# Query columns from a side-by-side head layout by SyncE, and an output projection in four quarters

## The chip, the cores and the metric

The kernel runs on one core of one Trainium2 chip. The metric is the time of one execution on the device in microseconds (us); shorter is better. A core has five instruction streams: TensorE (PE) multiplies matrices, VectorE (DVE) and ScalarE (ACT) do elementwise work, GpSimd (POOL) does small elementwise work and gathers, and SyncE (SP) only issues memory transfers (DMAs). Each stream runs in its own order; semaphores hold an instruction until what it needs is there. ACT and POOL can issue DMAs too, and an instruction that waits holds everything behind it on its engine.

## The reference

There are 64 sequences of 32 tokens with 512 features. Two residual layers are computed, all in float32:

```
W = weights[condition]                                  # 16 matrices of 32 x 32, one per sequence
x = x + einsum('bct,bcd->bdt', x, W)
q = rope(rmsnorm(x Wq^T)), k = rope(rmsnorm(x Wk^T)), v = x Wv^T      # 32 query heads, 8 key heads of 128
k_all = [k_cache[block_table] (512 keys), k],  v_all likewise         # 16 pages of 32 keys
scores = q k_all^T / sqrt(128); cached keys beyond the sequence's length are masked
x = x + (softmax(scores) v_all) Wo^T
```

## The kernel before, in words

Four sequences make a tile of 128 token rows, so there are 16 tiles. The 8 key heads are split in two halves of 4, and the kernel goes through all tiles for the first half and then for the second: 32 **steps**, numbered 0 to 31. A step has 4 **batches** (its sequences), a batch 4 **slots** (its key heads), so a step has slots 0 to 15. The second half adds to what the first half left in memory (`acc_d`).

A slot of attention is: `scores` (L806, 8 matmul records, an exponential on ACT into `pr`), and `values` of the slot before (L865, 8 matmul records into `po`). A slot with nothing else is called bare here. Slots 0, 1 and 3 of a step also do the 32 new keys (`new_scores` into `psn`, `new_values` into `pnv`).

Cached keys come as 16 pages a batch, one DMA of 64 KB each, issued by SP (`load_k`, L308) into one of two buffers `k_t`. DVE copies one head's keys at a time into `kh` (`head_keys`, L794), three slots ahead of its use. A buffer is free for the next batch but one when its fourth head is copied, which is the copy made in the batch's first slot. Cached values are gathered by POOL into `raw` and masked by ACT into `v` (L362).

Beside the attention of a step, the queries, keys and values of later tiles are made. From step 4 on, two tiles form a pair (`Pair`, L602), and the projections of both are computed together in block products (`products`, L661, seven products in place of eight, in the manner of Strassen and Winograd). There are three sets: set 0 (query heads 0 and 1) and set 1 (2 and 3) are made in the even step two steps ahead of the pair, set 2 (keys and values) in the odd step after. Each set has four parts, `p1_p6`, `p5_p2`, `p7` and `p4_p3`, and a list of four slots says where each stands (`where`, L1221). A set needs three sums of weights, `t2`, `t3` and `t4`, of 512 KB. They are made once in each half and then loaded by SP from `sums_d` for each pair (`load_sums`, L655), two buffers in turn (tile `t_x` in the profile). Each product's result goes through `norm_rope` (L466: squares on ACT, a reduction on DVE, a power on POOL, five more operations on DVE) and through a transposition on DVE in blocks (`turn_rows`, L513), and POOL writes it to memory (`heads_d`).

From there the rows come back as columns (`spread`, L524): one step ahead, 4 DMAs of 240 KB bring the first three batches' columns into `q_cols` and 4 DMAs of 80 KB the last batch's into `q_last` (two buffers). The `q_cols` DMAs are issued by ACT, the `q_last` DMAs by SP (`spread_of`, L1144). `q_cols` has one buffer, whose last reader is slot 11.

After a batch, DVE turns its output (`turn`, L899) into `ot`, and one step later the output projection multiplies `ot` with `Wo` in 16 matrix products (`out_proj`, L742), 8 in slot 8 and 8 in slot 9; DVE adds the result to the residual tile `res`, and SP stores it at slot 11 (`store`, L761).

The order of PE and of SP is the order of the program text, which the loop over steps and slots (L1283) and the table `plan` make; on DVE, ACT and POOL a scheduler of the framework places the instructions. In a slot the program has: the scores, the planned pieces, the output projection, the fetch of values, the values, and the key copies. A batch's key pages are issued at the start of the batch two ahead of it; those of the batch that starts in slot 12 are issued half there and half at slot 13. All DMAs of SP and ACT take eight semaphores in turn, in program order, and each DMA waits for the one eight before it.

## Time and profile before

| what | value |
|---|---|
| median of 3 runs | 2630.88 us (2629.29 to 2639.11) |
| the profiled execution's own time | 2618.95 us |
| its span, from the first to the last instruction | 2617.2 us |
| mean granted TensorE clock | 0.915 of full speed |
| DMA | 478.66 MB, mean 183 GB/s |
| key pages | 2048 DMAs of 64 KB by SP |
| weight sums loaded | 108 DMAs of 512 KB by SP |
| head rows written | 150 DMAs of 256 KB by POOL, 2.8 us to landing |
| columns loaded | 120 DMAs of 240 KB by ACT, 120 of 80 KB by SP |

How to read it. A line of the engine summary gives the busy time, its share of the span and the number of instructions; PEld is PE's weight load, which overlaps PE. A line of waits reads "engine line <- what it waited for: us in total, times, longest". SPq and ACTq are the parts of these engines that issue DMAs, which do not count as busy. A line of a timeline gives start and duration in us, engine, line of the kernel, operation, what it writes and reads (buffer numbers left out), the shape, how many instructions are merged, and in brackets how long the engine was idle before and what ended that. Where such a line names a DMA or an engine, it is the last of several semaphores that were waited for. A line of queues gives packets, MB and the time the packets took as a share of the 16 DMA engines' span; q1 belongs to SP, q10 to ACT, q0 to POOL. The profile is of one execution.

### The profile page before, as it was taken

What the parts mean: (1) busy time and instruction counts of PE and PEld (TensorE: products, weight loads), DVE (VectorE), ACT (ScalarE), POOL (GpSimd) and SP (SyncE); (2) the same over time, 40 slices, a digit from 0 to 9 for tenths busy, and PEclk for the clock granted to TensorE, in tenths of its full rate; (3) what the DMA queues carried; (4) which work ended last, traced back from release to release, by engine and by line L of the source; (5) the groups of instructions that cost most, each with busy time, mean ns of one, the idle gap of its engine ahead of it and who ended that gap; (6) DMA issues with size and microseconds to landing.
All of it is one profiled execution on the core that took longest, in us unless ns stands there. A gap on an engine that the chain in (4) does not pass through costs nothing.

```text
span 2617.2 us, 42090 instructions
## 1 busy us (share of the span) xinstructions
PE 2205.8 (84%) x12804; PEld 1546.5 (59%) x12804; DVE 1365.4 (52%) x3142; ACT 863.2 (33%) x1591; POOL 903.4 (35%) x1089
## 2 busy tenths in 40 slices
PE   8999888797887978878888797887978879788788
PEld 5765565565655656655565565665656656555566
DVE  4657756455464553745646355373453734537423
ACT  3442433233432333223333233332333323332242
POOL 3533434234342342423334233232332423324221
PEclk9999899898998988999889898898988989889989
DMA  7765665665656656676766865655656566565563
GB/s 223 216 180 171 194 201 171 176 199 176 195 165 179 197 170 193 203 223 177 217 180 187 217 184 170 184 163 173 193 167 190 163 175 191 166 183 162 165 182 95
DMA packets 485755, 478.66 MB, mean 183 GB/s; under 512 B 57072, under 2 KB 400496, under 8 KB 485520
## 3 DMA queue, kind: packets, MB, share of 16 engines
q1 hardware_dynamic: 368016, 262.22, 35.2%
q0 software_dynamic: 55088, 180.01, 21.9%
q10 hardware_dynamic: 62416, 33.64, 5.3%
q8 instruction: 105, 1.72, 0.3%
q14 instruction: 130, 1.06, 0.1%
HBM read 406.45 MB, written 69.21 MB: 182 GB/s over the span
## 4 chain that ended last, share of the span: by engine, by line
PE 55%; DMA 19%; SPq 10%; issue 5%; DVE 4%; ACT 2%; POOL 2%; ACTq 0%; POOLq 0%; DVEq 0%
PE pout_x L749 14%; PE ps_x L810 11%; PE po_x L871 11%; SPq L322 10%; PE pb_x L671 8%; DMA k_t_x<-in_kt_dram 6%; DMA t_x<-sums_d 6%; PE pc_x L671 5%; DMA q_cols_x<-heads_d 4%; PE pa_x L671 4%; PE pp_q_x L461 1%; DVE kh_x L803 1%; ACT sq_q_x L471 1%; PE psn_x L831 1%; DMA raw_x<-in_vc_dram,v_row 1%
## 5 line engine op out<-in xcount | busy, mean ns | idle before, releaser
L349 POOL DMA_INDIRECT raw_x<-in_vc_dram,v_row x512 | 540.9, 1057 | 937.9 <-ACT v_x L362 865.4
L871 PE MATMUL po_x<-v_x,pr_x 128*128 128x129 f32 x4088 | 584.4, 287 | 214.4 <-ACT pr_x L821 113.9
L871 PEld LDWEIGHTS po_x<-v_x,pr_x 128*128 128x128 f32 x4088 | 542.7, 200 | 351.1 <-issue 121.2
L821 ACT ACTIVATE pr_x<-ps_x 128x512 f32<-128x512 f32 x511 | 306.3, 599 | 1036.6 <-PE ps_x L810 1025.1
L749 PE MATMUL pout_x<-wo_x,ot_x 128*128 128x512 f32 x1024 | 450.1, 592 | 0.0
L810 PE MATMUL ps_x<-q_cols_x,kh_x 128*128 128x128 f32 x3064 | 420.5, 282 | 10.0 <-DMA q_cols_x<-heads_d 9.1
L362 ACT ACTIVATE v_x<-raw_x,valid 128x512 f32<-128x512 f32 x512 | 367.2, 721 | 144.6 <-DMA k_t_x<-in_kt_dram 51.8
L810 PEld LDWEIGHTS ps_x<-q_cols_x,kh_x 128*128 128x128 f32 x3064 | 387.7, 198 | 14.3 <-issue 13.5
L671 PE MATMUL pb_x<-t_x,x_x 128*128 128x512 f32 x432 | 245.2, 697 | 145.2 <-DMA t_x<-sums_d 145.1
L803 DVE COPY kh_x<-k_t_x 128x512 f32<-128x512 f32 x506 | 212.5, 421 | 256.3 <-PE ps_x L810 244.8
L749 PEld LDWEIGHTS pout_x<-wo_x,ot_x 128*128 128x128 f32 x1024 | 191.9, 190 | 228.2 <-issue 227.9
L671 PEld LDWEIGHTS pb_x<-t_x,x_x 128*128 128x128 f32 x432 | 87.3, 223 | 236.7 <-issue 226.0
L687 DVE TENSOR_TENSOR u_x<-pb_x,z_x 128x512 f32<-128x512 f32 x84 | 58.0, 691 | 291.1 <-PE pb_x L671 280.7
L478 POOL TENSOR_TENSOR rs_q_x<-ms_q_x,minus_half 128x4 f32<-128x4 f32 x128 | 143.2, 1119 | 154.6 <-DVE ms_q_x L476 153.3
L889 DVE TENSOR_TENSOR nv_x<-po_x,nv_x 128x258 f32<-128x258 f32 x256 | 107.0, 418 | 152.8 <-PE po_x L871 145.3
L475 DVE TENSOR_REDUCE ms_q_x<-sq_q_x 128x4 f32<-128x512 f32 x128 | 87.2, 681 | 157.8 <-ACT sq_q_x L471 157.5
L522 POOL DMA_DIRECT2D heads_d<-rows_x x150 | 91.0, 607 | 188.7 <-DVE rows_x L517 86.2
L810 PE MATMUL ps_x<-q_last_x,kh_x 128*128 128x128 f32 x1024 | 148.0, 292 | 0.0
L810 PEld LDWEIGHTS ps_x<-q_last_x,kh_x 128*128 128x128 f32 x1024 | 137.5, 209 | 0.0
L365 POOL COPY v_x<-valid 128x16 f32<-128x16 f32 x128 | 32.1, 251 | 265.2 <-PE po_x L871 265.0
L892 DVE TENSOR_TENSOR o_x<-nv_x,rden 128x256 f32<-128x256 f32 x256 | 107.5, 420 | 5.9
L671 PE MATMUL pc_x<-wq_x,x_x 128*128 128x512 f32 x224 | 105.9, 595 | 0.0
(180 smaller groups left out, 2126.5 us busy)
## 6 DMA issues: line engine op xcount, KB each, us to landing
k_t_x<-in_kt_dram SPq DMA_DIRECT2D x2048, 64.0 KB
t_x<-sums_d SPq DMA_DIRECT2D x108, 512.0 KB
heads_d<-rows_x POOLq DMA_DIRECT2D x150, 256.0 KB, 2.8
q_cols_x<-heads_d ACTq DMA_DIRECT2D x120, 240.0 KB
q_last_x<-heads_d SPq DMA_DIRECT2D x120, 80.0 KB
sums_d<-t SPq DMA_DIRECT2D x18, 512.0 KB
raw_x<-in_vc_dram,v_row POOLq DMA_INDIRECT x512, 4.0
wo_x<-in_wo_dram SPq DMA_DIRECT2D x32, 256.0 KB
```

The costliest lines, as they stand in the source:

```text
L322: ins = nc.sync.dma_start(k_raw[:, j, :, :].rearrange("p g r -> p (g r)"), kt[hh, bass.ds(page[j], 1)].rearrange("o d e -> (o d) e"),)
L349: nc.gpsimd.indirect_dma_start(out=raw.rearrange("p g d -> p (g d)"), out_offset=None, in_=vc, in_offset=bass.IndirectOffsetOnAxis(ap=v_ro ...
L362: nc.scalar.activation(v_bufs[b % 2][:, c, :, 0:D], raw, AF.Copy, scale=ok)
L478: nc.gpsimd.tensor_tensor(rs, ms, minus_half, ALU.pow)
L671: nc.tensor.matmul(bank, pair.x[:, i, c, :], w[:, c * 512 : (c + 1) * 512], start=start and c == 0, stop=c == 1, skip_group_check=not start,)
L749: nc.tensor.matmul(st.po, st.ot[:, i, :], wt["o", st.hh, i // 4][:, i % 4, :], start=(i == 0), stop=(i == QH - 1),)
L803: last["dve"] = nc.vector.tensor_copy(k, ba.k_raw[:, :, g, :]).ins
L810: nc.tensor.matmul(ps[:, c, :], ba.k[g][:, c * P : (c + 1) * P], queries(ba, g), start=True, stop=True,)
L821: last["act"] = nc.scalar.activation(pr, ps, AF.Exp, scale=SCALE).ins
L871: nc.tensor.matmul(ba.po[:, g % 2, :], ba.pr[g][:, c, :], ba.v_t[:, c, g, :], start=(c == 0), stop=(c == VC - 1),)
L889: nc.vector.tensor_tensor(t, ba.po, t, ALU.add)
L892: nc.vector.tensor_tensor(ba.o[:, both, :], t[:, :, 0:D], rd.unsqueeze(2).to_broadcast([P, 2, D]), ALU.mult,)
```

## The change

The memory layout of a step's heads changes from rows that hold four 128-element blocks of one head each to `[4, 128, 5, 128]`: for each of the four blocks, and for each of its 128 (batch, element) rows, the five heads (four query heads and the key head) stand side by side. POOL's write of one head becomes 128 x 4 pieces of 512 bytes in place of 128 rows of 2048. A column load becomes pieces of 5 x 512 = 2560 bytes in place of 512, and all of them are issued by SP: the `q_cols` loads move from ACT to SP.

The columns of a pair's first tile are now loaded in slot 14 (`q_cols`) and 15 (`q_last`) in place of 13 and 14, those of the second tile in slots 13 and 10 in place of 12 and 10. The sets move to slots 4, 6, 8, 9 (set 0), 11 to 14 (set 1) and 4, 6, 8, 11 (set 2), and loads of weight sums, of the pair's inputs and of weights move with them. From step 4 on the output projection goes in quarters into slots 5, 7, 8 and 10. The turning of the first two batches moves from slot 9 to 10, that of the third stays in slot 13, and the store moves from 11 to 13.

```diff
--- before.py
+++ after.py
@@ -198,7 +197,7 @@
         for hh in range(NHH)
     ]
     heads_d = [
-        dram.tile([HEAD_ROWS, 4 * P], F32, tag=f"heads_d{n}", name=f"heads_d{n}")
+        dram.tile([4, P, GH + 1, P], F32, tag=f"heads_d{n}", name=f"heads_d{n}")
         for n in range(NHH * NT)
     ]
 
@@ -378,8 +377,8 @@
             tag = "acc"
             if st.n in (2, 3, 5) and not exact:
                 tag = "sums"
-            elif st.n > 7 and not exact:
-                tag = ("u3", "u2")[st.n % 2]
+            elif st.n > 6 and st.n % 2 and not exact:
+                tag = "u3"
             st.acc = work.tile(
                 [P, HID], F32, tag=tag, name=f"acc_{st.name}", bufs=1 if tag[0] == "u" else 2
             )
@@ -518,21 +517,16 @@
                 part.rearrange("p k (h s) -> p h k s", h=4),
                 rd.rearrange("p h (k d) -> p h k d", k=4),
             )
-            rows = heads_d[st.n][i * S : i * S + (GH + 1) * P : GH + 1, :]
-            nc.gpsimd.dma_start(rows, part.rearrange("p k c -> p (k c)"))
-
-        def spread(st, b0, b1, eng):
-
-
-            whole_rows = heads_d[st.n]
+            nc.gpsimd.dma_start(heads_d[st.n][:, :, i, :].rearrange("k p c -> p k c"), part)
+
+        def spread(st, b0, b1):
+
+
+            src = heads_d[st.n].rearrange("k (b d) i c -> k d b (i c)", b=BT)
+            to = q_last[st.n % 2].unsqueeze(1) if b0 == BT - 1 else q_cols
+            to = to.rearrange("p b i c -> p b (i c)")
             for k in range(4):
-                src = bass.AP(
-                    tensor=whole_rows.tensor,
-                    offset=whole_rows.offset + b0 * (GH + 1) * S * 4 * P + k * P,
-                    ap=[[(GH + 1) * 4 * P, S], [S * 4 * P, (b1 - b0) * (GH + 1)], [1, P]],
-                )
-                to = q_last[st.n % 2] if b0 == BT - 1 else q_cols.rearrange("p b i c -> p (b i) c")
-                eng.dma_start(to[k * S : (k + 1) * S], src)
+                nc.sync.dma_start(to[k * S : (k + 1) * S], src[k][:, b0:b1, :])
 
         def by_tensor(st):
             return st.n < 2 or exact
@@ -693,7 +687,7 @@
             t = {}
 
             def p1_p6():
-                t[2], t[3] = made[pair.hh, k] if first else (pair.t[k, 0], pair.t[k, 1])
+                t[2] = made[pair.hh, k][0] if first else pair.t[k, 0]
                 b11, t["b21"], t[1], t["b22"] = halves(pair.hh, k)
                 t["a"], t["b"] = bank("pa"), bank("pb")
                 product(t["a"], A11, b11, True)
@@ -712,7 +706,7 @@
                 done(s0, e0, t["a"])
 
             def p7():
-                product(t["b"], S3, t[3])
+                product(t["b"], S3, made[pair.hh, k][1] if first else pair.t[k, 1])
                 t["u3"] = temp("u3")
                 add(t["u3"], t["b"], t["z"])
                 if e1[0] == "v":
@@ -1142,12 +1136,8 @@
                 at(n, slot, work_of)
 
         def spread_of(st, cols, last_cols):
-            def by_scalar():
-                with tc.issue_after(last["act"]):
-                    spread(st, 0, BT - 1, nc.scalar)
-
-            at(st.n - 1, cols, by_scalar)
-            at(st.n - 1, last_cols, lambda: spread(st, BT - 1, BT, nc.sync))
+            at(st.n - 1, cols, lambda: spread(st, 0, BT - 1))
+            at(st.n - 1, last_cols, lambda: spread(st, BT - 1, BT))
 
         def angles_of(m, n, slot):
             def angles():
@@ -1202,7 +1192,7 @@
             elif not pair.hh:
                 at(n - 1, 12, lambda pair=pair: pair_x(pair))
                 input_of(s0, n - 1, (n - 1, 9), (n - 1, 6), 12, 13)
-                input_of(s1, n - 1, (n - 1, 10 if n > 4 else 12), (n - 1, 7), 14, 15)
+                input_of(s1, n - 1, (n - 1, 11 if n > 4 else 12), (n - 1, 7), 14, 15)
                 at(n, 1, lambda pair=pair: sums_x(pair))
                 angles_of(s0.n // 2, n - 1, 9)
                 tables_of(pair, "q", n, 1)
@@ -1210,40 +1200,41 @@
             else:
                 at(
                     n - 1,
-                    10 if n < NT else 10,
+                    12,
                     lambda pair=pair: pair_x(pair),
                     lambda pair=pair: load_x(pair),
                 )
-                at(n - 1, 13, lambda pair=pair: sums_x(pair))
+                at(n, 1, lambda pair=pair: sums_x(pair))
                 tables_of(pair, "q", n - 1, 11)
                 tables_of(pair, "k", n + 1, 2)
             if early:
                 where = [(0, 2, (10, 11, 12, 14)), (1, 3, (4, 5, 6, 8)), (2, 3, (9, 10, 11, 12))]
             else:
                 where = [
-                    (0, n, (4, 5, 6, 8)),
-                    (1, n, (10, 11, 12, 14)),
-                    (2, n + 1, (4, 5, 6, 8)),
+                    (0, n, (4, 6, 8, 9)),
+                    (1, n, (11, 12, 13, 14)),
+                    (2, n + 1, (4, 6, 8, 11)),
                 ]
             for k, m, slots in where:
                 fresh = early or half_first
                 set_of(pair, k, m, slots, fresh)
                 if fresh:
-                    at(m, slots[0] - 2, lambda pair=pair, k=k: sums_w(pair.hh, k))
+                    before = 1 if k == 1 and not early else 2
+                    at(m, slots[0] - before, lambda pair=pair, k=k: sums_w(pair.hh, k))
                 else:
                     at(m, slots[0] - 2, lambda pair=pair, k=k: load_sums(pair, k, 0))
-                    at(m, slots[0] - 1, lambda pair=pair, k=k: load_sums(pair, k, 1))
-                    at(m, slots[1], lambda pair=pair, k=k: load_sums(pair, k, 2))
-            spread_of(s0, 13, 14)
-            spread_of(s1, 12, 10)
+                    at(m, slots[0] - (k != 1), lambda pair=pair, k=k: load_sums(pair, k, 1))
+                    at(m, slots[0] + 1, lambda pair=pair, k=k: load_sums(pair, k, 2))
+            spread_of(s0, 14, 15)
+            spread_of(s1, 13, 10)
         for i in range(2):
             for g in range(2):
-                at(NT - 4, 9 + 2 * g + i, lambda i=i, g=g: load_parts([("q", g)], 1, i))
+                at(NT - 4, 10 + 2 * g + i, lambda i=i, g=g: load_parts([("q", g)], 1, i))
         for j in range(4):
             g, i = 2 + j // 2, j % 2
             at(NT - 4 + (j > 0), 15 if j == 0 else j - 1, lambda g=g, i=i: load_parts([("q", g)], 1, i))
             kind = "kv"[j // 2]
-            at(NT - 3, 9 + j, lambda kind=kind, i=i: load_parts([(kind, 0)], 1, i))
+            at(NT - 3, 12 + j, lambda kind=kind, i=i: load_parts([(kind, 0)], 1, i))
 
         def count(hh):
 
@@ -1272,6 +1263,7 @@
         load_cond_weights(2)
         for part in (3, 4, 5):
             load_parts(outputs, 0, part)
+        out_parts = [{8: (0, 1), 9: (2, 3)}, {5: (0,), 7: (1,), 8: (2,), 10: (3,)}]
         second_outputs = {
             (0, 10): (0,),
             (1, 2): (1,),
@@ -1305,15 +1297,15 @@
                     kept.clear()
                     if slot == 3 and st.n > 2:
                         reload(steps[st.n - 1])
-                    if slot in (8, 9) and st.n:
-                        out_proj(steps[st.n - 1], slice((slot - 8) * QH // 2, (slot - 7) * QH // 2))
-                    if slot == 9:
+                    for part in out_parts[st.n > 3].get(slot, ()) if st.n else ():
+                        out_proj(steps[st.n - 1], slice(part * GH, (part + 1) * GH))
+                    if slot == 10:
                         if st.n:
                             new_ot(st)
                         for ba in turned:
                             turn(ba)
                         turned = []
-                    if slot == 11 and st.n:
+                    if slot == 13 and st.n:
                         store(steps[st.n - 1])
                     if slot == 13:
                         for load in after.pages_left if after else ():
@@ -1332,7 +1324,7 @@
                     if slot >= GH and valued is not None:
                         values(*valued)
                     valued = this, g
-                    if g == 1 and bt != 1:
+                    if g == 1 and bt in (0, BT - 1):
                         for ba in turned:
                             turn(ba)
                         turned = []
```

More of the change, by code (lines that the diff above doesn't have):

```diff
@@ L54 @@
 WARM = 10
-HEAD_ROWS = (GH + 1) * (P + S)
 TRIG = 2
```

## The prediction

> **What bounds the kernel now.** I read the page's busy times first, then the waits of PE and of SP, then the timelines of one pair of steps (20 and 21) engine by engine.
>
> ```profile
> PE 2205.8 (84%) x12804; PEld 1546.5 (59%) x12804; DVE 1365.4 (52%) x3142; ACT 863.2 (33%) x1591; POOL 903.4 (35%) x1089
> ...
> PE pb_x L671 <- DMA t_x<-sums_d: 145.1, 26, 11.3
> PE po_x L871 <- ACT pr_x L821: 113.9, 16, 11.3
> PE po_x L871 <- ACT v_x L362: 100.4, 15, 8.4
> ...
> SPq L322 <- DVE kh_x L803: 647.9, 84, 18.0
> ```
>
> PE is the bound, and its 411 us of idle time are nearly all in these three waits: 214.3 us on ACT (31 waits, 7 us each) and 145.1 us on weight sums. What ACT does meanwhile stands in its timeline; the first two lines are the end of odd step 19, the others even step 20:
>
> ```profile
> 1657.71 10.01 ACTq L535 DMA_DIRECT2D q_cols_x<-heads_d  x4
> 1667.77 0.72 ACT L362 ACTIVATE v_x<-raw_x,valid 128x512 f32<-128x512 f32 x1 [9.56 <-DMA k_t_x<-in_kt_dram]
> ...
> 1734.80 10.71 ACTq L535 DMA_DIRECT2D q_cols_x<-heads_d  x4
> 1745.61 0.63 ACT L471 ACTIVATE sq_q_x<-u_x 128x512 f32<-128x512 f32 x1 [10.24 <-DMA k_t_x<-in_kt_dram]
> ```
>
> Four column loads hold ACT for 10 us, though each issue takes 310 ns (median over the line's 120). The rest is waiting for the landing of key pages: ACT's loads stand in one order with SP's pages and cannot pass them. PE in the same two places, then at the next weight sum:
>
> ```profile
> 1669.03 2.09 PE L871 MATMUL po_x<-v_x,pr_x 128*128 128x129 f32 x8 [7.94 <-ACT pr_x L821]
> 1672.33 2.05 PE L810 MATMUL ps_x<-q_cols_x,kh_x 128*128 128x128 f32 x8 [1.22 <-DMA q_cols_x<-heads_d]
> ...
> 1746.91 0.80 PE L871 MATMUL po_x<-v_x,pr_x 128*128 128x129 f32 x2 [8.05 <-ACT v_x L362]
> ...
> 1778.62 3.75 PE L671 MATMUL pb_x<-t_x,x_x 128*128 128x512 f32 x4 [9.61 <-DMA t_x<-sums_d]
> ```
>
> So a pair has three stalls: B, at the end of the odd step (7.94 + 1.22); A, in slot 13 of the even step (8.05); C, in slot 4 of the next odd step (9.61). After each, the matmuls run at half speed for a while (x8 in 2.09 instead of 1.05). The pair repeats every 164 us. What C hangs on is in DVE's and SP's timelines:
>
> ```profile
> 1746.28 0.69 DVE L475 TENSOR_REDUCE ms_q_x<-sq_q_x 128x4 f32<-128x512 f32 x1 [4.94 <-ACT sq_q_x L471]
> ...
> 1761.92 0.40 DVE L803 COPY kh_x<-k_t_x 128x512 f32<-128x512 f32 x1
> ...
> 1770.61 0.91 SPq L456 DMA_DIRECT2D rot_k_x<-rot_dk  x2
> 1771.62 0.84 SPq L658 DMA_DIRECT2D t_x<-sums_d  x2
> ```
>
> DVE is behind with four rope chains; the key copy that frees the page buffer comes only at 1762.3. SP then issues 16 pages (8.3 us), two rope tables and the weight sum, which PE gets 7.0 us after its issue.
>
> **Part 1, stall A: column loads of odd steps, from ACT to SP.** I measure from the slot in which the second block set begins (scores at 1723.02, slot 10) to the end of C (1778.62): 55.6 us. In the new kernel this set begins in slot 11. Its PE work up to the next step is five slots, 5.2 + 5.2 + 3.5 + 5.2 + 1.8 = 20.9 us (bare slot 1.8, a pair of products 1.7, in the same timeline). But PE doesn't end the stretch. The built program's order for DVE has the same rope chains in front of the key copy that frees the buffer. In the old trace DVE runs from 1733.56 (first reduction of the set's ropes, 10.5 after the set's start) to 1762.32: 28.8 us, of which 4.94 waiting for ACT and 0.94 + 0.60 for POOL, so 22.3 of work. In the new order one key copy (0.4) now comes before this stretch and one addition and reciprocal (0.5) behind it: 21.4. With the two POOL waits kept the copy ends at 10.5 + 21.4 + 1.5 = 33.4 us, and C ends 16.3 us later (1762.32 to 1778.62), at 49.7. Since one bare slot now lies before the set, the gain is 55.6 - 49.7 - 1.8 = 4.1 us, not the 8 of the stall with its slow matmuls: PE is there at 20.9 + 13.2 (slots 0 to 4) = 34.1 and loses 15 us, some 3 at late key copies, which is new, and 12 in C. Bounds: if DVE catches up, PE alone sets the end, a gain of 19.7; if POOL's or ACT's answers cost DVE another 5 us, a loss of 1. I take 4.1, because the copy order is known and the ropes are the same. The new wait that the squeezed slots 11 to 14 could make, on the third weight sum behind 8 pages (4.2 us), is at most 2 us and lies before the same copy. Even steps 4 to 28 are 13; step 14 is followed by no load of sums and keeps all (its slots 13 and 14 last 7.5 and 7.6 us, against 3.5 and 5.2: 6.4). So 12 x 4.1 + 6.4 = 56.
>
> Step 30 has no products; its 8.4 us stall becomes a wait for columns behind 8 pages: 1.5 + 4.2 + 1.7 + 4.9 landing = 12.3 against 7.2 of PE work. Gain 11 - 5 = 6. Steps 2 and 3 stall 5.8 and 2.2 on ACT; I take half, 4.
>
> **Part 2, stall B: column loads of even steps.** Here SP issues them behind 16 pages. Before, from the scores of slot 12 (1654.67) to the first scores of step 20 (1672.33): 17.7 us for 7.2 us of PE work. After: key copy 1.5, 16 pages 8.4 to 10.0 (8.23 to 10.01 in the rows), output store 0.4, in the second half the two inputs of the next pair (now in slot 12) 0.9, four column loads at SP's median 0.43 = 1.7, landing 4.9 (1667.41 to 1672.33): 16.5 to 19.4. That is the old 17.7. ACT is free, but PE's next scores need these very columns. In the second half 0.75 MB more (inputs and store) lie before them, 3.7 us at the 202 GB/s of that stretch if nothing else gives; the larger pieces give about 1 back. I take +1 us for 7 odd ends and -1 us for 6: 1 us lost. Ends: -2 to +4 us for each of 15.
>
> ```profile
> 1655.00:1672.00 17.00, 8.17 (x63) 7.68 (x61) 4.19 (x11) 4.95 (x9) 4.89 (x6) 0.78 0.84 202
> ```
>
> (Stretch, its length, busy time of PE, weight loads, DVE, ACT, POOL, granted clock, DMA share, GB/s.)
>
> **Part 3, the pieces.**
>
> ```profile
> q1 hardware_dynamic: 368016, 262.22, 35.2%
> q0 software_dynamic: 55088, 180.01, 21.9%
> q10 hardware_dynamic: 62416, 33.64, 5.3%
> ```
>
> The ACT queue with its 512-byte pieces moves 33.64 MB in 5.3% of 2617, 242 GB/s; POOL's queue, with 2 KB rows, 314. The columns (39 MB) go from the first rate to the second or better, 162 to 125 us of all engines; the head writes, now 512 pieces of 512 bytes instead of 128 of 2 KB, go the other way by the same 37. Sum 0. POOL's issue of 512 pieces is shown by wk_x at 788 ns against 607: 150 x 0.18 = 27 us on an engine busy 35%. What hides it is POOL's idling; without that, a rope's power on POOL comes 0.2 us later, inside the 1.5 us above.
>
> SP gets 120 issues, 51 us, and waits 648 us for key copies, which hides them, except at B, where they are counted. The other moves (the later input by a slot, weight loads at the half change by one to three, weight sums by a slot, x4 issues each or fewer) stay in stretches where SP waits for key copies: 0, and without that cover 0.4 us for each issue, some 2 us a pair. The stores at slot 13 wait for nothing: the projection ends in slot 10. Turning two batches in slot 10 instead of 9 fits, since the projection first reads them in the next step.
>
> **Part 4, the projection in quarters.** 32 matmuls of 0.43 us either way, 13.7 us a step: 0 in PE time. It fills bare slots, so the key pages keep pace there; the old trace shows no PE wait for keys to win back. The price is that the first set's four ropes now end on the second set's heels; I counted about 4 us of DVE slack before the second set, so 0. Were it gone, each 1 us costs 12.
>
> **A rule against the change.** ACT's row is 10.01 us for four issues of 0.31. The Trainium skill, DMA: Bandwidth & Descriptors, section "Issuing engines are not separate DMA queues", says that queues of several engines share the same 16 DMA engines and that issuing from another one saves only sequencer time. By it the move would save ACT 1.24 us a step, none of it on PE's path, and the sum would be 0; by the row it also takes 9 us of waiting off ACT. For B I side with the rule's result, for A with the row.
>
> **Sum.** 56 + 6 + 4 - 1 = 65 us. The profiled execution took 2618.95 (span 2617.2), so 2554; the median of the three runs is 2630.88, 12 above it, so 2566.
>
> **Rivals.**
> - *DVE catches up* (0.17): without ACT's hold the ropes start early enough and C shrinks too; 3 to 6 us more in each of 13 pairs is 2566 - 39 to 78 = 2488 to 2527. Against it: 21 us of rope work in 20.9 us of slots.
> - *The change only moves the wait* (0.08): DVE's lag takes 5 us in each even step; 2618 to 2644.
> - *SP as the new neck, slower* (0.13): the columns wait in one in-order queue behind 16 pages, inputs and a store. From 5.2 us for each of 15 odd ends it is slower (65 gained and 13 of uncertainty); at 8 us it gives 2566 + 120 = 2686. For it: the DMA share is 0.84 there already. Against: SP has finished its pages at 1666.2, and ACT's last load went out at 1667.4, so the time is the same.
>
> **Numbers.** My forecast has 0.62, with a range of its own of 2527 to 2617. Faster by over 0.5%, which is about what a measurement tells from no change: 0.62 + 0.17 = 0.79; same 0.08; slower 0.13. The range 2505 to 2625 leaves out the slower case and the lower part of the first rival.
>
> **What will show it.** PE's waits on ACT pr_x and v_x fall from 214 us to under 60, and no ACT row is ended by a key page. PE's wait on t_x stays at 120 to 200, and on q_cols_x it rises from 9 to about 130, at the first scores of even steps. DVE's busy time stays near 1365. I am wrong if the odd ends grow beyond 21 us, if the key copies stop PE by more than 4 us in a pair beside C, or if C falls below 6.

## The result, and the profile after

The changed kernel takes 2622.23 us (median of 17 runs, 2612.49 to 2634.74); the kernel before, run beside it, 2628.55 us (17 runs, 2618.94 to 2639.11). The ratio is 0.9976 with a 95% interval of 0.9959 to 0.9994: 6 us less, and within the 0.5% that the prediction takes for no change, where 65 us less had been forecast. The profiled execution has a span of 2616.2 us (2617.2 before) and a mean granted clock of 0.922 (0.915 before).

The busy times and the queues of the page of the changed kernel:

```profile
PE 2187.8 (84%) x12804; PEld 1531.7 (59%) x12804; DVE 1363.4 (52%) x3142; ACT 863.4 (33%) x1591; POOL 916.2 (35%) x1089
...
q1 hardware_dynamic: 366096, 291.72, 39.1%
q0 software_dynamic: 55088, 180.01, 22.0%
q10 hardware_dynamic: 2896, 4.14, 0.4%
```

The columns have gone from ACT's queue (q10) to SP's (q1); together the two take 39.5% of the DMA engines' time, against 40.5% before. Busy times hardly move. The waits do (what waited, for what: us in total, times, longest), here PE's largest ones in the changed kernel:

```profile
PE ps_x L804 <- DMA q_cols_x<-heads_d: 182.8, 17, 18.9
PE pb_x L665 <- DMA t_x<-sums_d: 135.1, 31, 9.9
...
PE ps_x L804 <- DMA q_last_x<-heads_d: 24.5, 2, 12.3
PE ps_x L804 <- DVE kh_x L797: 24.2, 21, 1.8
```

The 214 us of waits on ACT are gone, the wait for weight sums is nearly as large as before (145.1), and a wait for columns has come, from 9 to 183 us. It sits at stall B, the end of the odd step. SP's timeline at the end of odd step 21 (start, duration, engine, line, operation, what goes where, how many merged):

```profile
1819.81 0.33 SPq L455 DMA_DIRECT2D rot_q_x<-rot_dq  x1
1821.51 4.63 SPq L321 DMA_DIRECT2D k_t_x<-in_kt_dram  x8
1826.55 0.54 SPq L612 DMA_DIRECT2D x_x<-x1t_d  x2
1827.15 0.42 SPq L756 DMA_DIRECT2D out_dram<-res_x  x1
1827.76 5.55 SPq L321 DMA_DIRECT2D k_t_x<-in_kt_dram  x8
1833.99 1.75 SPq L529 DMA_DIRECT2D q_cols_x<-heads_d  x4
1835.79 1.82 SPq L529 DMA_DIRECT2D q_last_x<-heads_d  x4
```

And PE in the same stretch, the scores of slot 12 and the first scores of step 22:

```profile
1818.78 1.06 PE L804 MATMUL ps_x<-q_last_x,kh_x 128*128 128x128 f32 x8
...
1840.76 2.04 PE L804 MATMUL ps_x<-q_cols_x,kh_x 128*128 128x128 f32 x8 [14.67 <-DMA q_cols_x<-heads_d]
```

One in-order queue issues 8 pages, two inputs, the store, 8 pages, and only then the columns that PE stands for: 22.0 us from slot 12 to the next step for 7.2 us of PE work. The packets in the trace follow that order: the last 512-byte packet of these pages ends at 1834.73, the first of the columns' packets (2560 bytes) starts at 1834.95, and those of `q_cols` and `q_last` together then run until 1841.04. ACT, which used to send the columns out among the pages, is idle. The DMA engines are not: in the middle of the stall (stretch, length, busy time of PE, weight loads, DVE, ACT, POOL, granted clock, DMA share, GB/s) they are 0.93 busy.

```profile
1827.80:1834.00 6.20, 0.00 (x0) 0.00 (x0) 1.50 (x4) 0.00 (x0) 0.00 (x0) 0.79 0.93 292
```

From PE's timelines I took, for the 13 pairs made in steps 4 to 29, the time from the start of set 1 to the end of C (the old one less the bare slot that now lies before the set), that of B (slot 12 of the odd step to the first scores of the next) and the pair's period, means in us:

| | set 1 to end of C | B | period of a pair |
|---|---|---|---|
| before | 54.8 - 1.8 = 53.0 | 17.8 | 164.5 |
| changed | 48.3 | 22.0 | 163.7 |

So 4.6 us a pair (60 in all) are gained where they were forecast, and 4.2 us (55 in all) are lost at B. By the starts of the steps, the whole is: steps 0 and 1 +7.6 us (step 2 now begins with a wait of 8.0 us for its columns, which SP sends too), steps 2 and 3 +0.9, steps 4 to 29 -10.4, steps 30 and 31 with the end +0.9; together the 1.0 us between the two spans.

### The profile page after: what moved, and what is told of

The parts are those of the page before. It is cut to its first block, busy times and chain, and to the rows that moved or that the text cites. A ratio compares the mean times of both kernels' runs of the same rounds, so it can differ in the third digit from the quotient of the medians.

```text
span 2616.2 us, 41964 instructions
## 1 busy us (share of the span) xinstructions
PE 2187.8 (84%) x12804; PEld 1531.7 (59%) x12804; DVE 1363.4 (52%) x3142; ACT 863.4 (33%) x1591; POOL 916.2 (35%) x1089
## 4 chain that ended last, share of the span: by engine, by line
PE 57%; DMA 15%; SPq 11%; DVE 8%; issue 6%; POOL 1%; ACT 1%; DVEq 0%; POOLq 0%; ACTq 0%
PE pout_x L743 17%; PE ps_x L804 11%; PE po_x L865 10%; SPq L321 9%; PE pb_x L665 8%; DMA t_x<-sums_d 5%; DMA q_cols_x<-heads_d 4%; PE pc_x L665 3%; PE pa_x L665 3%; DMA k_t_x<-in_kt_dram 3%; PE pp_q_x L460 1%; DVE kh_x L797 1%; DVE ms_q_x L474 1%; SPq L529 1%; DVE rope_q_x L496 1%
## 5 line engine op out<-in xcount | busy, mean ns | idle before, releaser
L348 POOL DMA_INDIRECT raw_x<-in_vc_dram,v_row x512 | 522.7, 1021 | 986.7 <-ACT v_x L361 922.7
L865 PEld LDWEIGHTS po_x<-v_x,pr_x 128*128 128x128 f32 x4088 | 537.2, 197 | 161.5 <-issue 152.5
L804 PE MATMUL ps_x<-q_cols_x,kh_x 128*128 128x128 f32 x3064 | 427.3, 284 | 241.5 <-DMA q_cols_x<-heads_d 182.8
L865 PE MATMUL po_x<-v_x,pr_x 128*128 128x129 f32 x4088 | 567.0, 283 | 0.7 <-ACT v_x L361 0.6
L743 PE MATMUL pout_x<-wo_x,ot_x 128*128 128x512 f32 x1024 | 459.4, 593 | 2.3 <-DMA wo_x<-in_wo_dram 2.3
L797 DVE COPY kh_x<-k_t_x 128x512 f32<-128x512 f32 x506 | 219.9, 436 | 420.6 <-PE ps_x L804 413.2
L665 PE MATMUL pb_x<-t_x,x_x 128*128 128x512 f32 x432 | 236.9, 676 | 141.2 <-DMA t_x<-sums_d 135.1
L520 POOL DMA_DIRECT2D heads_d<-rows_x x150 | 122.3, 816 | 148.7 <-DVE rows_x L516 83.5
L804 PE MATMUL ps_x<-q_last_x,kh_x 128*128 128x128 f32 x1024 | 135.2, 275 | 0.2 <-issue 0.2
L804 PEld LDWEIGHTS ps_x<-q_last_x,kh_x 128*128 128x128 f32 x1024 | 124.6, 192 | 0.4 <-issue 0.4
```

The source lines that it names most:

```text
L348: nc.gpsimd.indirect_dma_start(out=raw.rearrange("p g d -> p (g d)"), out_offset=None, in_=vc, in_offset=bass.IndirectOffsetOnAxis(ap=v_ro ...
L520: nc.gpsimd.dma_start(heads_d[st.n][:, :, i, :].rearrange("k p c -> p k c"), part)
L665: nc.tensor.matmul(bank, pair.x[:, i, c, :], w[:, c * 512 : (c + 1) * 512], start=start and c == 0, stop=c == 1, skip_group_check=not start,)
L743: nc.tensor.matmul(st.po, st.ot[:, i, :], wt["o", st.hh, i // 4][:, i % 4, :], start=(i == 0), stop=(i == QH - 1),)
L797: last["dve"] = nc.vector.tensor_copy(k, ba.k_raw[:, :, g, :]).ins
L804: nc.tensor.matmul(ps[:, c, :], ba.k[g][:, c * P : (c + 1) * P], queries(ba, g), start=True, stop=True,)
```

## The experiments

Ratios below are to the kernel before, run beside it on the same chip. The theory at this point, "order": B has grown because the columns stand behind work that nobody needs yet, in SP's one queue. Its first rival, "bandwidth": the bytes of the burst have to be moved before the step can go on, whatever their order.

### Even steps' columns from ACT again

```diff
-            spread_of(s0, 14, 15)
+            def by_scalar(s0=s0):
+                with tc.issue_after(last["act"]):
+                    spread(s0, 0, BT - 1, nc.scalar)
+            at(s0.n - 1, 13, by_scalar)
+            at(s0.n - 1, 15, lambda s0=s0: spread(s0, BT - 1, BT))
```

> The changed kernel with one thing put back: the q_cols loads of even steps (slot 13 of an odd step) are issued by ACT again, those of odd steps stay on SP; new layout, new sets, new quarters stay. Theory 'order': stall B grew because the columns now stand behind 16 pages, the inputs and the store in SP's one queue; from ACT's own stream they go out beside the pages as before, so slot 12 to the next step's first scores falls from 22.0 us to about 17.8, and 13 ends x 4.2 = 55 us come off: about 2567. Rival 'bandwidth' (the inputs and the store lie before the columns, the DMA engines are full): the ends stay at 21 to 23 and the time at 2610 to 2630. Rival 'layout' (the new pieces are slower to land): the same as bandwidth, with a landing of over 6 us after the last issue.

Measured: 2574.42 us, ratio 0.9806 (0.977 to 0.9843). B is 16.7 us in the mean. ACT at the end of odd step 21, whose slot 12 begins at 1791.89:

```profile
1794.94 7.35 ACTq L529 DMA_DIRECT2D q_cols_x<-heads_d  x4
```

and PE's first scores of step 22:

```profile
1807.34 2.04 PE L804 MATMUL ps_x<-q_cols_x,kh_x 128*128 128x128 f32 x8 [1.66 <-DMA k_t_x<-in_kt_dram]
```

SP issues 16 pages, inputs and a store in the same stretch as in the changed kernel (1794.58 to 1807.19), but the columns go out beside them and PE resumes 15.4 us after slot 12 in place of 22.0. With the one engine put back, the forecast (2566) nearly comes out. The layout is the new one here, so it isn't what made B longer; nor is it the late first page, which comes 2.6 us after slot 12 here as in the changed kernel. The slot of the loads has moved with the engine, from 14 to 13; the next run moves the slot alone.

### Columns between the two halves of the pages

```diff
-            spread_of(s0, 14, 15)
+            spread_of(s0, 13, 15)
```

> The changed kernel with the q_cols loads of even steps one slot earlier (13 in place of 14), so in SP's order they come after 8 of the 16 pages. Theory 'order': first page 2.7 us after slot 12's scores, 8 pages 4.6, inputs 0.9, four columns 1.7, landing 5.4 = 15.3 in place of 22.0; 13 x 6.7 = 87 off, 2535, less what the 8 pages pushed back cost later (key copies wait or C grows: up to 2 us a pair, 26). Rival 'bandwidth': the burst takes as long in any order, the ends stay above 20 or the stall comes back as a wait for key pages in slots 1 to 4; 2605 to 2630.

Measured: 2619.39 us, ratio 0.9978 (0.9959 to 0.9997): nothing, against the theory's 2535. SP at the end of step 21 (slot 12 begins at 1825.97):

```profile
1828.69 4.38 SPq L321 DMA_DIRECT2D k_t_x<-in_kt_dram  x8
1833.16 0.86 SPq L612 DMA_DIRECT2D x_x<-x1t_d  x2
1834.20 2.01 SPq L529 DMA_DIRECT2D q_cols_x<-heads_d  x4
1836.25 0.72 SPq L756 DMA_DIRECT2D out_dram<-res_x  x1
1837.16 9.57 SPq L321 DMA_DIRECT2D k_t_x<-in_kt_dram  x8
```

The columns go out 7 us earlier, and PE resumes at 1846.10, 20.1 us after slot 12. From their issue to that moment the columns take 10 us instead of 5.4, and the 8 pages behind them 9.57 us to issue instead of 5.55, since each DMA waits for the one eight before it (SP's waits for `q_cols` ahead of page loads are 77.0 us in all, 38.4 in the changed kernel). A window over that time:

```profile
1833.00:1846.00 13.00, 0.28 (x3) 0.08 (x1) 1.52 (x4) 0.74 (x2) 1.39 (x2) 0.60 0.94 247
```

So the rival is right within the burst: it is full, and what is issued into it waits for what was issued before. In the trace's DMA packets the first 8 pages end at 1835.85, the two inputs at 1839.99 and the columns at 1844.95, 1.15 us before PE resumes; of the 8 pages behind them 269 of 1024 packets have moved by then. So the columns waited for the pages and inputs ahead of them, not for the whole burst. (PE's wait goes by the name of key pages in this run, `k_t_x`, 136.1 us in all. But scores read only `q_cols` or `q_last` and `kh`, so it is a wait for columns, under the name of another DMA that takes the same semaphore in turn.)

In the mean B falls by 2.3 us, to 19.7. These don't reach the total, since the even step takes 1.7 us longer up to set 1: its new scores now wait for `q_last`, 48.8 us in all against 3.4 in the changed kernel.

```profile
PE psn_x L825 <- DMA q_last_x<-heads_d: 48.8, 15, 7.4
```

What the run doesn't tell is whether columns issued before the burst must wait for it.

### Columns ahead of all pages

```diff
-            spread_of(s0, 14, 15)
+            at(s0.n - 1, 11.5, lambda s0=s0: spread(s0, 0, BT - 1))
+            at(s0.n - 1, 15, lambda s0=s0: spread(s0, BT - 1, BT))
...
                 n = st.n * BT + bt + 2
+                for piece in plan.get((st.n, bt * GH - 0.5), ()):
+                    piece()
```

> The changed kernel with the q_cols loads of even steps ahead of all 16 pages in SP's order (right after slot 11, when their buffer is free), q_last at slot 15. Theory 'order': the columns land some 7 us after slot 12's scores, which is what PE needs for the four slots, so the end takes 7.5 to 10 us in place of 22.0: 13 x 12 = 156 off at most; I expect 60 to 156 off, 2466 to 2562, since the next waits are the weight sums of set 0 (loaded from slot 2 of the even step) and C. Rival 'bandwidth': what B loses comes back as waits for key pages or weight sums at the start of the even step; 2600 to 2630.

Measured: 2567.92 us, ratio 0.977 (0.9748 to 0.9793), 6 us short of the theory's range and far from the rival's. B is 9.2 us. The next wait is one that I had overlooked: the new scores in slot 0 read the last batch's columns too, which were still at the end of the queue.

```profile
1816.13 0.39 PE L825 MATMUL psn_x<-q_last_x 128*32 128x128 f32 x1 [9.94 <-DMA q_last_x<-heads_d]
```

### Rope tables later

The tables of the next pair's query ropes stand in slot 11, ahead of the pages, and their buffer is freed by a rope on DVE. In SP's waits of the changed kernel:

```profile
SPq L455 <- DVE ropeu_k_x L488: 72.9, 8, 10.9
```

```diff
-                tables_of(pair, "q", n - 1, 11)
+                tables_of(pair, "q", n - 1, 15)
```

> The changed kernel with the loads of the q rope tables in slot 15 in place of 11 of odd steps (second half only). In the trace of the changed kernel these loads hold SP until a rope on DVE frees their buffer, and the 16 pages and the columns stand behind them. Theory 'order': first page 1.2 us earlier than 2.7, 7 odd ends x 1.2 to 2.7 = 8 to 19 us off, 2603 to 2614. Rival: SP would wait for the key copy that frees the page buffer anyway, and nothing comes off: 2617 to 2627.

Measured: 2612.89 us, ratio 0.9945 (0.9922 to 0.9968). B falls from 22.0 to 21.6. The interval touches that of the changed kernel; at most some 9 us lie here. Most of those 73 us of SP's wait are spent waiting for the key copy instead, whose wait grows from 608.8 to 684.1 us.

### Both columns first

```diff
-            spread_of(s0, 14, 15)
+            spread_of(s0, 11.5, 10)
-                tables_of(pair, "q", n - 1, 11)
+                tables_of(pair, "q", n - 1, 15)
```

(with the loop's two lines from above)

> The changed kernel with both column loads of even steps ahead of the 16 pages in SP's order: q_last in slot 10, q_cols right after slot 11, and the q rope tables in slot 15. In the run with q_cols alone moved ahead, the new wait was 138.8 us of PE's new scores on q_last, which stood at the end of the queue. Theory 'order': that wait goes too, the ends take 8 to 10 us and slot 0 of even steps about 5 in place of 14; 2568 - 139 = 2429, and up to 70 us of it may come back at weight sums and late key pages: 2430 to 2500. Rival 'bandwidth' (the burst of pages, inputs, store and columns has to be moved before the step can go on): slots 1 to 4 of even steps wait for key pages and the time stays at 2550 to 2575.

Measured: 2552.08 us, ratio 0.973 (0.9677 to 0.9783): the rival's figure, but hardly by its mechanism: pages that come late reach PE as late key copies, and PE's waits for these (`kh_x`) are 41.9 us in all, against 24.2 in the changed kernel. B is gone (7.1 us in the second half, which is PE's work; 9.3 in the first, whose slots hold more), and in its place PE waits for weight sums in even steps too, 222.4 us in all (114.6 of them in slot 4 of even steps, 25.8 in the changed kernel). SP after the start of step 22 (1791.92):

```profile
1801.85 8.93 SPq L321 DMA_DIRECT2D k_t_x<-in_kt_dram  x16
1810.82 0.90 SPq L652 DMA_DIRECT2D t_x<-sums_d  x2
```

PE:

```profile
1814.92 3.44 PE L665 MATMUL pb_x<-t_x,x_x 128*128 128x512 f32 x4 [8.73 <-DMA t_x<-sums_d]
```

The same form again: the sums, in slots 2 and 3, stand behind slot 0's 16 pages, which are for a batch eight slots away. The prediction had put C, the same stall in odd steps, down to DVE's rope chains, since they make the key copy late and with it the pages. The next two runs tell the two readings apart: if DVE is the limit, sums loaded earlier only turn C into waits for keys.

### Weight sums ahead of slot 0's pages

```diff
-                    at(m, slots[0] - 2, lambda pair=pair, k=k: load_sums(pair, k, 0))
-                    at(m, slots[0] - (k != 1), lambda pair=pair, k=k: load_sums(pair, k, 1))
+                    at(m, slots[0] - 2 if k == 1 else -0.5, lambda pair=pair, k=k: load_sums(pair, k, 0))
+                    at(m, slots[0] if k == 1 else -0.5, lambda pair=pair, k=k: load_sums(pair, k, 1))
```

In the changed kernel, with the columns left as they are there (and the loop's two lines from above):

> The changed kernel with t2 and t3 of sets 0 and 2 loaded ahead of slot 0's pages; the columns stay behind the pages of slot 12 as in the changed kernel. Theory 'order': C goes (some 9 us in slot 4 of odd steps, 135 us of waits on weight sums in all) and B stays at 22: 2622 - 60 to 117 = 2505 to 2562. Rival 'DVE': what C loses comes back as waits for key copies, 2600 to 2630.

and in the kernel with both columns first:

> The run with both columns first (2552 us), and t2 and t3 of sets 0 and 2 loaded ahead of the 16 pages of slot 0 in place of slots 2 and 3. In that run PE waits 222.4 us for weight sums, some 9 us in slot 4 of each step, while the sums stand behind slot 0's pages in SP's queue. Theory 'order' (each of the stalls A to D is a load that stands behind pages which nobody needs yet): both waits go, 9 + 8 us a pair or more; 13 pairs x 17 = 221, of which I expect 100 to 221 to stay: 2330 to 2450. Rival 'DVE' (the prediction's step: C hangs on DVE's rope chains, which delay the key copy): PE then waits for key copies in slots 4 to 8 instead, as they are late by the same time, and the time stays above 2500.

Measured: the sums alone 2461.64 us, ratio 0.9356 (0.932 to 0.9393); columns and sums 2286.09 us, ratio 0.8706 (0.8664 to 0.8748). Both are faster than the theory expected: a pair takes 151.7 us with the sums alone, 12.0 less than in the changed kernel, of which 7.9 lie before set 2's first sum is used. Another 3.0 lie between the start of the even step and set 1, where the sums of set 0 come ahead of the pages too. What follows a stall is part of this: four products with a sum take 1.88 us in the kernel with columns and sums first, and 3.44 after the stall above. With the sums alone, PE's waits are:

```profile
PE ps_x L804 <- DMA q_cols_x<-heads_d: 163.9, 13, 17.9
...
PE ps_x L804 <- DVE kh_x L797: 24.5, 21, 1.8
```

C is gone, B is what it was (21.9 us a pair), and the wait for key copies is the same as in the changed kernel (24.2): DVE's lag costs PE nothing more. With both, the page and PE's waits read:

```profile
PE 2133.3 (94%) x12804; PEld 1502.2 (66%) x12804; DVE 1363.2 (60%) x3142; ACT 864.7 (38%) x1591; POOL 918.7 (40%) x1089
```

```profile
PE ps_x L804 <- DVE kh_x L797: 27.4, 21, 4.3
PE ps_x L804 <- DMA q_cols_x<-heads_d: 26.7, 4, 9.3
...
PE pb_x L665 <- DMA t_x<-sums_d: 12.4, 9, 2.9
```

A pair takes 137.4 us in place of 163.7. The two moves together (336 us) bring more than the sum of each alone (161 and 70): with the columns alone, part of what B gives back is lost again at the weight sums of even steps.

### The engine alone, in the old kernel

```diff
-                    spread(st, 0, BT - 1, nc.scalar)
+                    spread(st, 0, BT - 1, nc.sync)
```

> The kernel before with the q_cols loads issued by SP in the slots they had (13 of odd steps, 12 of even ones); old layout, sets and halves. Theory 'order': stall A goes (4 us a pair) and the columns stand between the two halves of the pages in SP's queue, where they landed 10 us after their issue in the run with slot 13; odd ends 18 to 20 in place of 17.8: 2580 to 2620. Rival: without the moved sets nothing is gained at A, since the third weight sum then waits in the same queue: 2620 to 2650.

Measured: 2572.07 us, ratio 0.9788 (0.975 to 0.9825), better than both expectations. Set 1 to the end of C takes 47.1 us (48.9 less the bare slot), B 18.2. PE's waits there:

```profile
PE ps_x L810 <- DMA k_t_x<-in_kt_dram: 143.9, 15, 12.5
PE pb_x L671 <- DMA t_x<-sums_d: 88.3, 19, 10.1
PE ps_x L810 <- DMA q_cols_x<-heads_d: 75.5, 13, 11.9
```

The first and the third line are both waits for columns, as explained above; 74 us of them stand at the start of odd steps, whose columns SP now issues too. A goes and C shrinks (77.5 us of waits for sums in slot 4 of odd steps, 114.2 before), and B stays nearly as it was (17.8 before); here the inputs are loaded in slot 10 and the columns go out before the second 8 pages, which was not taken apart further. With all the rest of the change added the kernel is 50 us slower than with this one edit.

### Layout alone, halves again

In the kernel before, `heads_d`, its write and `spread` take the new layout, with ACT still issuing:

> The kernel before with the new layout of the heads alone (POOL writes 512-byte pieces, columns load in 2560-byte pieces), with ACT's loads, the slots and the halves as they were. The prediction costed this at 0: 2620 to 2635. Rival 'larger pieces land sooner': ACT's hold in slots 12 and 13 stays, as it waits for pages, but the columns land up to 1 us earlier at 15 odd ends: 2605 to 2620. Rival 'smaller writes': POOL's 0.2 us for each of 150 writes delays ropes: up to 2655.

In the changed kernel:

```diff
-        out_parts = [{8: (0, 1), 9: (2, 3)}, {5: (0,), 7: (1,), 8: (2,), 10: (3,)}]
+        out_parts = [{8: (0, 1), 9: (2, 3)}, {8: (0, 1), 9: (2, 3)}]
```

> The changed kernel with the output projection in halves in slots 8 and 9 again; everything else stays. The prediction costed the quarters at 0, with a slack of some 4 us on DVE before the second set, and 12 us for each us if that is gone. If so: 2615 to 2630. Rival: the quarters keep PE at work while SP fetches pages, and halves cost 1 to 3 us a step in bare slots: 2640 to 2700. Rival: the quarters squeeze the sets' ropes on DVE, and halves are faster: 2580 to 2610.

Measured: layout alone 2621.68 us, ratio 0.9974 (0.9945 to 1.0004); halves 2618.26 us, ratio 0.997 (0.9941 to 0.9999). Neither differs from its kernel by what can be told. POOL's issue does take longer, 816 ns in the mean where 788 was forecast and 607 measured before, in the page of the changed kernel:

```profile
L520 POOL DMA_DIRECT2D heads_d<-rows_x x150 | 122.3, 816 | 148.7 <-DVE rows_x L516 83.5
```

### The same two without the stalls, and the old sets

The edits of "columns and sums first" in the kernel before, all on SP, with old layout, sets and halves:

> The kernel before with old layout, old sets and halves, in which SP issues all column loads, those of even steps ahead of slot 12's pages (q_last in slot 10), the q rope tables come in slot 15, and t2 and t3 of sets 0 and 2 come ahead of slot 0's pages. This is the queue order alone, without the other parts of the change. If the queue order is what matters, it is within 30 us of the run with columns and sums first in the changed kernel; if the moved sets, the quarters or the layout add something once the queue is out of the way, it is 30 to 100 us slower than that run.

"Columns and sums first" with halves in slots 8 and 9, by the edit above:

> The run with columns and sums first, with the output projection in halves in slots 8 and 9. The prediction costed the quarters at 0, and halves cost nothing in the changed kernel (2618 against 2622), where stalls gave slack all round. If that price holds where PE is 94% busy: 2280 to 2295. Rival: the quarters spread PE's work so that key copies and ropes keep pace, which the stalls had hidden: halves cost 1 to 4 us a step, 2310 to 2400.

and with the old layout:

> The run with columns and sums first, with the heads in the old layout (rows of 2048 bytes written, columns loaded in 512-byte pieces). The prediction costed the layout at 0: 2275 to 2295. Rival: with PE 94% busy the DMA engines are nearer their limit (209 GB/s over the span in place of 183), and 512-byte columns, which moved at 242 GB/s in the kernel before, hold up pages and sums: 2300 to 2350.

Measured, in this order: 2443.55 us, ratio 0.9299 (0.9261 to 0.9336); 2331.62 us, ratio 0.8881 (0.884 to 0.8922); 2288.63 us, ratio 0.872 (0.8678 to 0.8762). The layout is worth nothing here either. The quarters, worth nothing in the changed kernel, are worth 45 us once the stalls are gone. PE's wait for key copies with halves, against 27.4 us with quarters:

```profile
PE ps_x L804 <- DVE kh_x L797: 71.4, 45, 3.5
```

The old sets are 157 us slower than the new ones, where 100 at most had been expected. Of these, 45 belong to the quarters and 3 to the layout; the rest, some 110, is left for the moved sets and loads. No run took back the sets alone, so this is a difference and not a measurement. The trace of the kernel with the old sets puts the wait at the third weight sum, which was not moved ahead (100.2 us in slot 8):

```profile
PE pb_x L671 <- DMA t_x<-sums_d: 103.6, 25, 11.5
```

### The rule at the places left

```diff
-        spread_of(steps[2], 12, 11)
-        spread_of(steps[3], 13, 14)
+        spread_of(steps[2], 11.5, 10)
+        spread_of(steps[3], 11.5, 10)
...
-            spread_of(s1, 13, 10)
+            spread_of(s1, 11.5 if s1 is steps[-1] else 13, 10)
...
-            (1, 2): (1,),
-            (1, 4): (2,),
-            (1, 5): (3, 4),
-            (1, 6): (5, 6),
+            (0, 12): (1,),
+            (0, 14): (2,),
+            (1, 2): (3,),
+            (1, 4): (4,),
+            (1, 5): (5,),
+            (1, 6): (6,),
```

> The run with columns and sums first (2286 us), with the same rule at the places that are left in its trace: the columns of steps 2, 3 and 31 ahead of slot 12's pages too, and the output weights of the second half loaded one to three slots earlier in steps 16 and 17. PE's waits there were 8.3, 8.4 and 9.3 us for columns and 8.1 and 2.5 for output weights, 37 us in all; I expect 15 to 35 of them to go: 2251 to 2271. Rival: the start and the end are bound by inputs that come later anyway, and nothing goes: 2280 to 2290.

Measured: 2267.78 us, ratio 0.864 (0.8596 to 0.8684). This is inside the 2251 to 2271 us that were expected, and over 13% faster than both kernels. The profiled execution has a mean granted clock of 0.976, and its page reads:

```profile
PE 2131.8 (94%) x12804; PEld 1498.5 (66%) x12804; DVE 1363.7 (60%) x3142; ACT 866.3 (38%) x1591; POOL 922.7 (41%) x1089
```

## Why the prediction was wrong, step by step

**Part 1, stall A and C: right in size.** From set 1's start to the end of C 49.7 us were predicted and 48.3 measured; the gain is 4.6 us a pair instead of 4.1, 60 us instead of 56. The total is partly luck, as two misses cancel in it: the twelve ordinary pairs gain 5.0 us each instead of 4.1, and the pair of step 14, for which 6.4 had been entered, gains nothing (41.9 us before, without the bare slot, and 42.1 after: slots 13 and 14 are short as forecast, but slots 1 and 3 of step 15 grow by 1.6 and 4.2). PE's waits on ACT fell to next to nothing, the wait on weight sums stayed (135.1, forecast 120 to 200), DVE's busy time too (1363.4, forecast 1365). PE waits 8.6 us at C in the mean, where a loss of 12 had been taken. The chain behind it, late key copy, then pages, then sums, was read rightly. What was wrong was to treat its last link as given: the sums can be issued before the pages, and then DVE's lag costs PE nothing. The rival "DVE catches up" looked for C's cure in DVE, which isn't where it lay.

**Steps 30, 2 and 3: wrong, small.** A gain of 6 us was forecast for step 30 and one of 4 for steps 2 and 3. Step 30 gained 0.4 and step 31 with the end lost 1.3; steps 2 and 3 lost 0.9. In step 30 the sum gave 12.3 us from slot 12 to the next step, and 17.3 were measured: its columns land late as they do at B. The 7.6 us lost before step 2 are in no term.

**Part 2, stall B: the step that failed.** The sum gave 16.5 to 19.4 us and called that the old 17.7; measured are 22.0. (Its short end leaves out the store, which the first half has too: by its own terms it is 16.9.) The sentence that led there is the one that SP had finished its pages at 1666.2 and ACT's last load went out at 1667.4, "so the time is the same". SP's rows there, before the change:

```profile
1656.21 10.01 SPq L322 DMA_DIRECT2D k_t_x<-in_kt_dram  x16
1666.41 2.74 SPq L535 DMA_DIRECT2D q_last_x<-heads_d  x4
```

The sentence took the old end of the two streams, which ran side by side, for the end of the new one, in which all columns are issued after the pages. Means over the ends of steps 15 to 29, in us after slot 12's scores (DMAs by the start of their issue):

| | first page | 16th page | first column load | last column load | next scores |
|---|---|---|---|---|---|
| before | 1.5 | 12.3 | 3.0 | 12.9 | 17.2 |
| changed | 2.6 | 14.3 | 15.0 | 16.3 | 21.7 |
| ACT issues again | 2.6 | 15.3 | 3.0 | 11.2 | 16.0 |
| columns between the page halves | 2.6 | 20.6 | 8.2 | 10.0 | 20.2 |
| both columns first | 2.1 | 13.8 | -4.1 | -2.6 | 7.2 |

Term by term, against the long end of the sum: the first page comes 2.6 us after slot 12 and not 1.5; the 16 pages with inputs and store take 12.0, to the end of the last issue, and not 10.0 + 0.4 + 0.9 = 11.3; the first column load is issued another 0.3 us later, for which there was no term; and from the start of the last column load PE resumes after 5.4 us (6.3 in the first half) where 4.9 had been taken. In the first half, which has no inputs there, the sum gave 18.5 at its long end and 22.6 were measured. Each miss is small; nearly all have the same sign, as all of it now stands in one line. B grew by 4.2 us, just beyond the -2 to +4 stated for an end; PE's wait on `q_cols_x`, forecast to reach about 130 us, reached 183. Stall B passed the 21 us that the prediction itself had named as the sign that it is wrong. The run in which ACT issues these loads again gives the 4.2 us back, and more (16.7).

**The rule.** For A the prediction sided with ACT's row, rightly. For B it sided with the rule's result, and that failed: the Trainium skill, DMA: Bandwidth & Descriptors, section "Issuing engines are not separate DMA queues", says that all engines' DMAs run on the same 16 DMA engines and that starting them from several saves only the sequencer's time. The first half agrees with the full burst (DMA share 0.93 above). The second does not hold here: putting four loads per odd end back on ACT takes 1.75 us of issuing off SP at each end and 48 us off the kernel's median, because the engine also decides behind what a load stands. The same page, in its section "Queues, rings and completion order", says that a DMA engine takes turns between the queues that have work for it; no run here tells such sharing from the mere order of issue.

**The third rival** (SP as the new neck) named the mechanism and its tipping point, 5.2 us an end. At 4.2 us it took the gain and left the time where it was.

**Parts 3 and 4.** Both zeros hold in this kernel (layout alone 0.9974, halves 2618 against 2622). For the layout it holds without the stalls too. For the quarters it was the stalls that made it zero, 45 us without them.

## What to carry to other kernels

When a load is moved from one engine's queue to another's, write down the new queue's order around it and ask of every entry ahead of it whether anybody needs that entry sooner; the sum of the issue times is not enough. Put the few loads that the next matmul needs ahead of the bulk that is prefetched for later, before the burst begins rather than in its middle: ahead of it they were free, in the middle the total gained nothing. And remove all such stalls before pricing the rest, since a part that is worth nothing beside a stall (the quarters) can be worth 2% without it.

## What the runs showed of the hardware

- How long a column load takes depends on what is in flight: from the last issue to PE's resumption 5.4 us behind the pages, 10 us in the middle of them, at a DMA share of 0.94 and 247 GB/s. In the latter case 8 pages and two inputs, issued before, were still on the move when the columns were issued at 1834.20; the columns' packets end at 1844.95, before 755 of the 1024 packets of the pages issued behind them.
- With fewer waits the same matmuls take less time. PE's busy time fell from 2205.8 us (mean granted clock 0.915) to 2131.8 (0.976) with the same 12804 records; the first scores after a stall take 2.04 us instead of 1.06.
- The mean rate of the DMAs is 210 GB/s with columns and sums first, against 183 before, for the same 478.65 MB: the DMA engines were full in bursts, and over the whole span there was room.
